# Node tiles in staged groups of four with index work behind them, an accumulator that holds x, and a selector multiplied in four pieces

## Chip, core and metric

The kernel runs on one core of a Trainium2 chip. The metric is device time in microseconds of one launch. Before the change it is 4528.94 us, the median of 10 runs (4525.16 to 4532.39). The names of the engines in the profile: PE multiplies matrices (PEld loads its weights), DVE is the vector engine, ACT the scalar engine, POOL is GpSimd, SP only issues DMAs. SP, ACT and POOL each have queues for DMAs.

## The reference

A layer of a graph network on 12,500 nodes (160 features: 64 scalars and 32 vectors of 3) and 400,000 edges, sorted by destination. Cut to what matters:

```
h  = max(layernorm(x), 0)
y0 = h[:, :64] @ W_l1_0 * a / 8 ;  y1 = einsum('nuc,uv->nvc', h1, W_l1_1) * a / sqrt(32)
s0, s1 = the same with W_sc0, W_sc1          # a: one factor per node
w  = silu(edge_features @ fc_W1 / 4) @ fc_W2 / 8    # 192 weights per edge
mid_a = w_a*y0[src]*e0 ; mid_d = w_d*sum_c(y1[src]*e1)/sqrt(3)
mid_b = (w_b*y0[src])[:, :, None]*e1 ; mid_c = (w_c*e0)[:, :, None]*y1[src]
z0, z1 = sums of mid over the edges of each destination / sqrt(10)
out = x + C_S*s + C_X*(z @ W_l2 * a / sqrt(96))
```

## The kernel before

The program has four parts in a row. Line numbers are those of the profile.

**Index work (L93 to L152).** Edges come in 3125 tiles of 128, three tiles to a window and four windows to a group (261 groups). `dst` is loaded and turned into floats (L103), the smallest destination of each window is found by a reduction (L107) and a POOL reduction over partitions (L112), and from that come the base tile of each group (`tile_i`), the positions `at`, and `drel`, the destination within its window (L114 to L149, all on DVE). A second POOL reduction (L151) makes `far_i`, which says whether a slow path for far destinations must run; with this data it is not entered. Weights are loaded by ACT's queue and scaled on DVE (L156 to L192).

**Node tiles (L220 to L256).** 98 tiles of 128 nodes in groups of 7. Per tile: row statistics on DVE (L231, L232), normalization on DVE (L240 for scalars, L242 for vectors, which are put in the order component, channel), two transposes on PE (L246, L247), the Relu in the copies out of PSUM (L249 on ACT, L250 on DVE), two matmuls against `wn0` and `wn1`, which hold both weight matrices side by side (L252, L253), and two copies: `yb` on ACT with the factor a (L254), and the other half into `acc` on DVE (L255). `yb` is written to `y_d` in DRAM by SP's queue (L256). A scheduler of the framework orders this part on each engine.

**Edges (L277 to L464).** The order is written out by hand, in steps b of four edge tiles (782 steps). `load` issues the gathers on POOL, one indirect DMA for each edge tile (L310), eight steps ahead, into ten buffers `yg`. `weigh` makes the edge weights (L341 on PE, L262 and L263 on ACT). `products` multiplies them with the gathered rows on DVE (L268 to L275). `select` makes, once per group, the 0/1 selector of 12 tiles (L364) and its three copies times the edge's vector (L366, 1152 elements per partition). `sums` multiplies selector and products on PE (L385). `turn`, `linear` and `add` (L400, L409, L421) take a finished group through the output weights, and `accumulate` adds the result to two neighbouring tiles of `acc`, whose number is read from `tile_i` into a register (L426 to L429).

**Output (L558 to L566).** All of x is loaded again, `acc` is multiplied by a on ACT (L562), and added to x on DVE in two instructions (L563, and L565 with the vector order undone); ACT's queue writes the rows.

Of the kernel before, what the change touches and what calls it, by code (L numbers as in the profile page):

```python
# [10 lines left out]
F32 = mybir.dt.float32  # L11
# [23 lines left out]
GN = 7  # L35
# [6 lines left out]
def kernel(  # L42
# [45 lines left out]
    nc.vector.memset(eps, EPS)  # L88

# [4 lines left out]
    nc.sync.dma_start(src_sb, src)  # L94
# [3 lines left out]
    far_i = const.tile([P, 1], I32, name="far_i")  # L98
    full = T // WT
    with tc.tile_pool(name="idx", bufs=1) as ip:  # L100
        dst_i = ip.tile([P, TP], I32, name="dst_i")
        nc.sync.dma_start(dst_i, dst)
        nc.vector.tensor_copy(drel, dst_i)  # L103
        neg = ip.tile([P, NG * GW], F32, name="neg")
# [6 lines left out]
        negb = ip.tile([P, NG * GW], F32, name="negb")  # L111
        nc.gpsimd.partition_all_reduce(negb, neg, P, bass_isa.ReduceOp.max)  # L112
        first = ip.tile([P, NG], F32, name="first")
# [36 lines left out]
        farb = ip.tile([P, 1], F32, name="farb")  # L150
        nc.gpsimd.partition_all_reduce(farb, far, P, bass_isa.ReduceOp.max)  # L151
        nc.vector.tensor_copy(far_i, farb)  # L152
# [3 lines left out]
    w1 = const.tile([P, 2 * FC_H], F32, name="w1")  # L156
    nc.vector.memset(w1, 0.0)
    for i in range(P // FC_IN):
        nc.scalar.dma_start(w1[FC_IN * i:FC_IN * (i + 1), FC_H * (i % 2):FC_H * (i % 2 + 1)], fc_w1)
    w2 = const.tile([P, NW], F32, name="w2")  # L160
    for i in range(2):
        for to, of, m in ((0, 0, M0), (M0, 2 * M0, M1), (M0 + M1, M0, M0), (2 * M0 + M1, 2 * M0 + M1, M1)):
            nc.scalar.dma_start(w2[FC_H * i:FC_H * (i + 1), to:to + m], fc_w2[:, of:of + m])
    nc.vector.tensor_scalar(w2, w2, 1.0 / math.sqrt(FC_H), None, ALU.mult)

    wn0 = const.tile([M0, 2, M0], F32, name="wn0")
    nc.scalar.dma_start(wn0[:, 0, :], w_l1_0)
    nc.scalar.dma_start(wn0[:, 1, :], w_sc0)
    nc.vector.tensor_scalar(wn0[:, 0, :], wn0[:, 0, :], 1.0 / math.sqrt(M0), None, ALU.mult)
    nc.vector.tensor_scalar(wn0[:, 1, :], wn0[:, 1, :], C_S / math.sqrt(M0), None, ALU.mult)  # L170
    wn1 = const.tile([3 * M1, 2, 3 * M1], F32, name="wn1")
    nc.vector.memset(wn1, 0.0)
    for c in range(3):
        s = slice(M1 * c, M1 * (c + 1))
        nc.scalar.dma_start(wn1[s, 0, s], w_l1_1)
        nc.scalar.dma_start(wn1[s, 1, s], w_sc1)
    nc.vector.tensor_scalar(wn1[:, 0, :], wn1[:, 0, :], 1.0 / math.sqrt(M1), None, ALU.mult)
    nc.vector.tensor_scalar(wn1[:, 1, :], wn1[:, 1, :], C_S / math.sqrt(M1), None, ALU.mult)

    wo = const.tile([P, 3, D], F32, name="wo")  # L180
    nc.vector.memset(wo, 0.0)

    def o1(c):
        return slice(M0 + M1 * c, M0 + M1 * (c + 1))

    nc.scalar.dma_start(wo[0:M0 + M1, 0, 0:M0], w_l2_0)
    for rows, k, c in ((slice(96, P), 0, 0), (slice(0, 32), 1, 1), (slice(32, 64), 1, 2)):
        nc.scalar.dma_start(wo[rows, k, o1(c)], w_l2_1[M0:, :])
    for rows, k, c in ((slice(64, P), 1, 0), (slice(0, 64), 2, 1), (slice(64, P), 2, 2)):
        nc.scalar.dma_start(wo[rows, k, o1(c)], w_l2_1[0:M0, :])  # L190
    nc.vector.tensor_scalar(wo[M0:M0 + M1, 0, 0:M0], wo[M0:M0 + M1, 0, 0:M0], 1.0 / math.sqrt(3.0), None, ALU.mult)
    nc.vector.tensor_scalar(wo, wo, C_X / math.sqrt(10.0 * (M0 + M1)), None, ALU.mult)  # L192
# [3 lines left out]
    nc.sync.dma_start(a_sb, attr)  # L196

# [3 lines left out]
    def node_dma(g, n, dma):  # L201

        f = min(g + n, N // P) - g
        if f:
            dma(slice(g * P, (g + f) * P), slice(0, f), P)
        if f < n:
            dma(slice((g + f) * P, N), slice(f, f + 1), N - (g + f) * P)
# [5 lines left out]
    def load_x(pool, g, n):  # L213
        xt = pool.tile([P, GN, D], F32, name="xt")
        if g + n == NT and N % P:
            nc.vector.memset(xt[:, n - 1, :], 0.0)
        node_dma(g, n, lambda rows, t, p: nc.sync.dma_start(xt[:p, t, :], by_tile(x[rows, :])))  # L217
        return xt

    with (  # L220
        tc.tile_pool(name="nx", bufs=4) as nx,
        tc.tile_pool(name="nd", bufs=3) as nd,
        tc.tile_pool(name="nd_pt", bufs=3, space=PSUM) as nd_pt,
        tc.tile_pool(name="nd_po", bufs=3, space=PSUM) as nd_po,
    ):
        for g, n in groups:
            xt = load_x(nx, g, n)
            st = nd.tile([P, GN, 6], F32, name="st")
            mv = nd.tile([P, GN, 2], F32, name="mv")
            for j in range(n):  # L230
                nc.vector.bn_stats(st[:, j, :], xt[:, j, :])  # L231
                nc.vector.bn_aggr(mv[:, j, :], st[:, j, :])  # L232
            rstd = nd.tile([P, GN], F32, name="rstd")
            nc.scalar.activation(rstd[:, :n], mv[:, :n, 1], AF.Sqrt, bias=eps)
            nc.vector.reciprocal(rstd[:, :n], rstd[:, :n])
            yb = nd.tile([P, GN, D], F32, name="yb")
            for j in range(n):
                i = g + j
                h = nd.tile([P, D], F32, name="h")
                nc.vector.tensor_scalar(h[:, 0:M0], xt[:, j, 0:M0], mv[:, j, 0:1], rstd[:, j:j + 1],  # L240
                                        ALU.subtract, ALU.mult)
                nc.vector.tensor_scalar(h[:, M0:].rearrange("p (c u) -> p c u", c=3),  # L242
                                        xt[:, j, M0:].rearrange("p (u c) -> p c u", c=3),
                                        mv[:, j, 0:1], rstd[:, j:j + 1], ALU.subtract, ALU.mult)
                pt = nd_pt.tile([P, 2, P], F32, name="pt")
                nc.tensor.transpose(pt[0:M0, 0, :], h[:, 0:M0], ident)  # L246
                nc.tensor.transpose(pt[0:3 * M1, 1, :], h[:, M0:], ident)  # L247
                hT = nd.tile([P, 2, P], F32, name="hT")
                nc.scalar.activation(hT[0:M0, 0, :], pt[0:M0, 0, :], AF.Relu)  # L249
                nc.vector.tensor_scalar(hT[0:3 * M1, 1, :], pt[0:3 * M1, 1, :], 0.0, None, ALU.max)  # L250
                po = nd_po.tile([P, 2, D], F32, name="po")
                nc.tensor.matmul(po[:, :, 0:M0], hT[0:M0, 0, :], wn0, start=True, stop=True)  # L252
                nc.tensor.matmul(po[:, :, M0:], hT[0:3 * M1, 1, :], wn1, start=True, stop=True)  # L253
                nc.scalar.activation(yb[:, j, :], po[:, 0, :], AF.Copy, scale=a_sb[:, i:i + 1])  # L254
                nc.vector.tensor_copy(acc[:, i, :], po[:, 1, :])  # L255
            node_dma(g, n, lambda rows, t, p: nc.sync.dma_start(by_tile(y_d[rows, :]), yb[:p, t, :]))  # L256
# [20 lines left out]
    with (  # L277
        tc.tile_pool(name="ld", bufs=2) as ld,
        tc.tile_pool(name="yg", bufs=10) as ygp,
        tc.tile_pool(name="hid", bufs=4) as hid,  # L280
        tc.tile_pool(name="prod", bufs=3) as prod,
        tc.tile_pool(name="selp", bufs=3) as selp,
# [75 lines left out]
        def select(g):  # L358

            ev = e4_group(g)  # L360
            lo, hi = g * TG, min((g + 1) * TG, T)
            n = hi - lo
            sel = selp.tile([P, TG, 4, WN], F32, name="sel")
            nc.vector.tensor_tensor(sel[:, :n, 3, :], iota[:, 0:WN].unsqueeze(1).to_broadcast([P, n, WN]),  # L364
                                    drel[:, lo:hi].unsqueeze(2).to_broadcast([P, n, WN]), ALU.is_equal)
            nc.vector.tensor_tensor(sel[:, :n, 0:3, :], sel[:, :n, 3:4, :].to_broadcast([P, n, 3, WN]),  # L366
                                    ev[:, :n, 1:4].unsqueeze(3).to_broadcast([P, n, 3, WN]), ALU.mult)
            sels[g] = sel
# [55 lines left out]
        def accumulate(g):  # L424
# [3 lines left out]
            to = acc[:, ds(i, 2), :]  # L428
            nc.vector.tensor_tensor(to, to, ps, ALU.add)  # L429
# [39 lines left out]
    with (  # L469
# [11 lines left out]
        with tc.For_i(0, n, 1) as _:  # L481
# [61 lines left out]
            with tc.For_i(0, NT, 1) as i:  # L543
# [11 lines left out]
                nc.vector.tensor_tensor(to, to, po.unsqueeze(1), ALU.add)  # L555


    with tc.tile_pool(name="fx", bufs=6) as fx:  # L558
        for g, n in groups:
            xt = load_x(fx, g, n)  # L560
            for j in range(n):
                nc.scalar.activation(acc[:, g + j, :], acc[:, g + j, :], AF.Copy, scale=a_sb[:, g + j:g + j + 1])  # L562
            nc.vector.tensor_add(xt[:, :n, 0:M0], xt[:, :n, 0:M0], acc[:, g:g + n, 0:M0])  # L563
            xv = xt[:, :n, M0:].rearrange("p t (u c) -> p t u c", c=3)
            nc.vector.tensor_add(xv, xv, acc[:, g:g + n, M0:].rearrange("p t (c u) -> p t u c", c=3))  # L565
            node_dma(g, n, lambda rows, t, p: nc.scalar.dma_start(by_tile(out[rows, :]), xt[:p, t, :]))  # L566
# [42 lines left out]
```

## Time and profile before

The profiled execution took 4524.6 us, of which its span, from first to last instruction, is 4522.7.

| | busy us | share | instructions |
|---|---|---|---|
| PE | 3544.0 | 78% | 17263 |
| DVE | 2791.1 | 62% | 6412 |
| ACT | 2567.4 | 57% | 9298 |
| POOL | 3230.5 | 71% | 3135 |

Busy time is an average over the four parts. The part with gathers runs from 284 to 4458 us, so what holds there is read from the rows of that stretch; the DMA engines moved 72 GB/s over the span and are far from full outside the last part. [...] Idle time "<-issue" is time in which an engine waited for nothing that the profile shows.

### The profile page before, as it was taken

Reading aid. Unit: us, or ns where it says so; the run is one execution under the profiler, and the core shown is the slowest. Engines: PE = TensorE matmul, PEld = TensorE weight load, DVE = VectorE, ACT = ScalarE, POOL = GpSimd, SP = SyncE. Lnnn points to the kernel's source line nnn. Section 1 sums busy time; section 2 is a strip of 40 time slices with the busy share of each in tenths; the row PEclk is TensorE's granted clock in tenths of the full one; section 3 lists DMA queues with packets and bytes.
Section 4 is the critical chain, followed back from the end, with each engine's and each line's share of the span. In section 5 each row is a group of like instructions: output and inputs, shape, how many; then the busy total and the mean of one; then the engine's idle time right before and its main releaser. Section 6 shows DMA issues by size and latency. Waiting matters only on the chain. (4 is left out here: it accounts for less than half of the span.)

```text
span 4522.7 us, 60313 instructions
## 1 busy us (share of the span) xinstructions
PE 3544.0 (78%) x17263; PEld 2454.8 (54%) x17263; DVE 2791.1 (62%) x6412; ACT 2567.4 (57%) x9298; POOL 3230.5 (71%) x3135
## 2 busy tenths in 40 slices
PE   4888887887787878787787777878878787877883
PEld 3555555555555555555555555555555555555552
DVE  6656666666666666666666666666666666666665
ACT  1245655655565556565655556555655565556555
POOL 0037777777777777777777777777777777777773
PEclk9999989899999999999989999889999999999997
DMA  2222222222222222222222222222222222222225
GB/s 82 71 61 71 71 69 69 70 68 71 69 71 71 70 69 71 68 71 71 69 70 71 69 70 71 68 70 69 72 71 70 69 71 68 71 70 69 70 67 170
DMA packets 245943, 327.78 MB, mean 72 GB/s; under 512 B 66040, under 2 KB 195352, under 8 KB 245352
## 3 DMA queue, kind: packets, MB, share of 16 engines
q0 software_dynamic: 150000, 256.20, 23.7%
q1 hardware_dynamic: 81030, 59.43, 4.5%
q10 hardware_dynamic: 14578, 8.25, 0.6%
q8 instruction: 141, 2.31, 0.2%
q14 instruction: 194, 1.59, 0.1%
HBM read 307.62 MB, written 16.00 MB: 72 GB/s over the span
## 5 line engine op out<-in xcount | busy, mean ns | idle before, releaser
L310 POOL DMA_INDIRECT yg<-y_d,src_sb x3125 | 3222.7, 1031 | 1188.0 <-issue 924.0
L385 PE MATMUL pz<-pr,sel 128*128 128x256 f32 x6250 | 1713.3, 422 | 678.6 <-DVE pr L275 676.6
L385 PEld LDWEIGHTS pz<-pr,sel 128*128 128x128 f32 x6250 | 1249.7, 210 | 955.1 <-DVE pr L275 545.6
L268 DVE TENSOR_TENSOR tmp<-yg,ev 128x384 f32<-128x384 f32 x782 | 436.3, 558 | 1544.4 <-DMA yg<-y_d,src_sb 1540.9
L262 ACT ACTIVATE wt<-pw,ev 128x96 f32<-128x96 f32 x3125 | 808.7, 344 | 324.3 <-ACT zs L392 213.6
L390 ACT ACTIVATE zs<-pz 32x192 f32<-32x192 f32 x1042 | 336.9, 323 | 1006.8 <-PE pz L385 999.8
L341 PE MATMUL pw<-w,hT 64*128 64x192 f32 x6250 | 778.6, 371 | 0.2 <-ACT wt L263 0.2
L341 PEld LDWEIGHTS pw<-w,hT 64*128 64x128 f32 x6250 | 532.6, 200 | 397.0 <-issue 395.9
L392 ACT ACTIVATE zs<-pz 32x64 f32<-32x64 f32 x3126 | 667.5, 214 | 41.6
L270 DVE TENSOR_REDUCE tmp<-tmp 128x128 f32<-128x384 f32 x782 | 463.8, 593 | 27.1
L319 PE MATMUL px<-xe,w 32*128 32x512 f32 x782 | 338.4, 710 | 158.1 <-DVE acc L429 156.8
L273 DVE TENSOR_TENSOR pr<-wt,yg 128x384 f32<-128x384 f32 x782 | 430.3, 550 | 0.0
L324 ACT ACTIVATE hT<-px 128x512 f32<-128x512 f32 x391 | 219.3, 595 | 343.1 <-PE px L319 339.7
L263 ACT ACTIVATE wt<-pw 128x384 f32<-128x384 f32 x782 | 398.9, 510 | 0.0
L366 DVE TENSOR_TENSOR sel<-sel,ev 128x1152 f32<-128x1152 f32 (+1 forms) x261 | 353.7, 1355 | 14.3 <-DMA ev<-in_e 5.4
L271 DVE TENSOR_TENSOR pr<-wt,yg 128x256 f32<-128x256 f32 x782 | 326.1, 417 | 0.0
L272 DVE TENSOR_TENSOR pr<-wt,yg 128x256 f32<-128x256 f32 x782 | 326.0, 417 | 0.0
L409 PE MATMUL px<-wo,za 128*128 128x160 f32 x1566 | 283.1, 317 | 0.4 <-ACT za L402 0.4
L409 PEld LDWEIGHTS px<-wo,za 128*128 128x128 f32 x1566 | 220.2, 190 | 60.1 <-ACT zs L392 33.7
L319 PEld LDWEIGHTS px<-xe,w 32*128 32x128 f32 x782 | 86.2, 201 | 285.9 <-DVE acc L429 210.0
L275 DVE TENSOR_TENSOR pr<-wt,tmp 128x128 f32<-128x128 f32 x782 | 223.2, 285 | 0.0
L421 PE MATMUL px<-os,place 128*128 128x160 f32 x1044 | 214.5, 328 | 0.4 <-ACT os L411 0.4
(78 smaller groups left out, 1736.9 us busy)
## 6 DMA issues: line engine op xcount, KB each, us to landing
yg<-y_d,src_sb POOLq DMA_INDIRECT x3125
xe<-in_e SPq DMA_DIRECT2D x784, 32.0 KB
xt<-in_x SPq DMA_DIRECT2D x26, 560.0 KB
y_d<-yb SPq DMA_DIRECT2D x13, 560.0 KB
out<-xt ACTq DMA_DIRECT2D x13, 560.0 KB
ev<-in_e SPq DMA_DIRECT2D x32, 192.0 KB
src_sb<-in_src SPq DMA_DIRECT2D x1, 1568.0 KB
dst_i<-in_dst SPq DMA_DIRECT2D x1, 1568.0 KB
```

What stands on the lines that cost most here:

```text
L262: nc.scalar.activation(wt[:, k, 0:96], pw[:, k, 0:96], AF.Copy, scale=ev[:, k, 0:1])
L263: nc.scalar.activation(wt[:, :n, 96:NW], pw[:, :n, 96:NW], AF.Copy)
L268: nc.vector.tensor_tensor(tmp[:, :n, 0:3, :], y1, ev[:, :n, 1:4].unsqueeze(3).to_broadcast([P, n, 3, M1]), ALU.mult)
L270: nc.vector.tensor_reduce(tmp[:, :n, 3, :], tmp[:, :n, 0:3, :].rearrange("p t c u -> p t u c"), AX.X, ALU.add)
L273: nc.vector.tensor_mul(pr[:, :n, 96:192].rearrange("p t (c u) -> p t c u", c=3), wt[:, :n, M0:96].unsqueeze(2).to_broadcast([P, n, 3, M1]) ...
L310: nc.gpsimd.indirect_dma_start(out=yg[:, k, :], out_offset=None, in_=y_d, in_offset=bass.IndirectOffsetOnAxis(ap=src_sb[:, t:t + 1], axis=0))
L319: nc.tensor.matmul(ph, w1[r, :], xe[r, :], start=True, stop=True)
L341: nc.tensor.matmul(pw[:, k, 0:NW], hT[r, o:o + P], w2[r, :], start=True, stop=True)
L366: nc.vector.tensor_tensor(sel[:, :n, 0:3, :], sel[:, :n, 3:4, :].to_broadcast([P, n, 3, WN]), ev[:, :n, 1:4].unsqueeze(3).to_broadcast([P, ...
L385: nc.tensor.matmul(pz[:, 0:PC], sels[g][:, t % TG, :, :], pr[:, k, :], start=t % WT == 0, stop=last)
L392: nc.scalar.activation(zs[:, 192 + M0 * c:192 + M0 * (c + 1)], pz[WN * c:WN * (c + 1), 192:PC], AF.Copy)
L409: nc.tensor.matmul(po[:m, :], za[:, k, :m], wo[:, k, :], start=k == 0, stop=k == 2)
```

## The change

Five things. The node part becomes stages of four tiles with an order written by hand (`center`, `leave`, `map_rows`, `turn_rows` of four different stages in one iteration, 25 stages); the normalization is split, so that ACT subtracts the mean with the Relu, and the factor 1/deviation, times a, comes at the very end. The index work and the edge weights move: x is loaded first, the first index pass is done in stage 6, and the rest after the last stage. `acc` starts as x + a s in the order of the output (the weights' columns are permuted), sums are added with the factor a, and the output part is DMAs alone, on two queues. The second POOL reduction becomes a matmul. The selector's multiplication runs in four pieces of three tiles. The pools `selp` and `prod` are made first.

```diff
-GN = 7
+GN = 8
+HN = 4
...
+        def center(q):
+            for k in range(n):
+                nc.vector.bn_stats(st[:, k, :], xt[:, j + k, :])
+                nc.vector.bn_aggr(mv[:, k, :], st[:, k, :])
+            nc.vector.tensor_scalar(nm[:, :n], mv[:, :n, 0], -1.0, None, ALU.mult)
+            for k in range(n):
+                nc.scalar.activation(h[:, k, :], xt[:, j + k, :], AF.Relu, bias=nm[:, k:k + 1])
+            nc.scalar.activation(ra[:, :n], mv[:, :n, 1], AF.Sqrt, bias=eps)
+        def turn_rows(q):
+            nc.vector.reciprocal(ra[:, :n], ra[:, :n])
+            nc.vector.tensor_mul(ra[:, :n], ra[:, :n], a_sb[:, g + j:g + j + n])
+            for k in range(n):
+                nc.tensor.transpose(pt[0:M0, 0, k, :], h[:, k, 0:M0], ident)
+                nc.tensor.transpose(pt[0:3 * M1, 1, k, :], h[:, k, M0:], ident)
+        def map_rows(q):
+            nc.scalar.activation(hT[0:M0, 0, :n, :], pt[0:M0, 0, :n, :], AF.Copy)
+            nc.vector.tensor_copy(hT[0:3 * M1, 1, :n, :], pt[0:3 * M1, 1, :n, :])
+            for k in range(n):
+                nc.tensor.matmul(po[:, :, 0:M0], hT[0:M0, 0, k, :], wn0, start=True, stop=True)
+                nc.tensor.matmul(po[:, :, M0:], hT[0:3 * M1, 1, k, :], wn1, start=True, stop=True)
+        def leave(q):
+            for k, po in enumerate(pos):
+                nc.scalar.activation(yb[:, j + k, :], po[:, 0, :], AF.Copy, scale=ra[:, k:k + 1])
+                nc.vector.scalar_tensor_tensor(acc[:, g + j + k, :], po[:, 1, :], ra[:, k:k + 1], xt[:, j + k, :],
+                                               op0=ALU.mult, op1=ALU.add)
...
+            for g, n in groups[:2]:
+                load_x(g, n)
+            nc.sync.dma_start(a_sb, attr)
+            node_weights()
+            nc.sync.dma_start(dst_i, dst)
...
+            for q in range(len(parts) + 3):
...
+                if q == min(2, last):
+                    edge_weight_loads()
+                if q == min(6, last):
+                    first_nodes()
+                if q <= last:
+                    center(q)
+                if 0 <= q - 3 <= last:
+                    leave(q - 3)
+                if 0 <= q - 2 <= last:
+                    map_rows(q - 2)
+                if 0 <= q - 1 <= last:
+                    turn_rows(q - 1)
+            edge_weights()
+            relate(pt[0:1, 0, 0, 0:1])
...
-            nc.vector.tensor_tensor(sel[:, :n, 0:3, :], sel[:, :n, 3:4, :].to_broadcast([P, n, 3, WN]),
-                                    ev[:, :n, 1:4].unsqueeze(3).to_broadcast([P, n, 3, WN]), ALU.mult)
+            for t in range(0, n, WT):
+                m = min(WT, n - t)
+                nc.vector.tensor_tensor(sel[:, t:t + m, 0:3, :], sel[:, t:t + m, 3:4, :].to_broadcast([P, m, 3, WN]),
+                                        ev[:, t:t + m, 1:4].unsqueeze(3).to_broadcast([P, m, 3, WN]), ALU.mult)
...
-            to = acc[:, ds(i, 2), :]
-            nc.vector.tensor_tensor(to, to, ps, ALU.add)
+            for h in range(2):
+                to = acc[:, ds(i + h, 1), :]
+                nc.vector.scalar_tensor_tensor(to, ps[:, h:h + 1, :], a_sb[:, ds(i + h, 1)], to,
+                                               op0=ALU.mult, op1=ALU.add)
...
-    with tc.tile_pool(name="fx", bufs=6) as fx:
-        for g, n in groups:
-            xt = load_x(fx, g, n)
...
+    for i, (g, n) in enumerate(groups):
+        eng = (nc.sync, nc.scalar)[i % 2]
+        node_dma(g, n, lambda rows, t, p: eng.dma_start(by_tile(out[rows, :]), acc[:p, g + t.start:g + t.stop, :]))
```

`first_nodes` holds L103 to L112 of before, `relate` the rest of the index work with the same instructions, `edge_weight_loads` the 23 loads of the edge part's weights on SP's queue, `edge_weights` their scalings on DVE. In the iteration each name is called for its stage: statistics and Relu of q, transposes of q − 1, copies and matmuls of q − 2, results of q − 3, whose second half of eight tiles also issues the write of `yb` to `y_d` on the queue of ACT.

## The prediction

> **What bounds the kernel now.** I read the stages first. In the table by stretch, each row is a stretch of the span with its length, then busy us (and instructions) of PE, weight loads, DVE, ACT, POOL, the clock column, DMA share and GB/s. The borders come from the timeline: first row statistics of a node tile at 52.36, last `yb` ended at 281.51, first gather at 284.08, last gather ended at 4458.46, first `xt` load of the closing loop at 4469.92.
>
> ```profile
> 0.00:52.30 52.30, 0.00 (x0) 0.00 (x0) 33.29 (x42) 0.00 (x0) 7.88 (x10) 1.00 0.26 85
> 52.30:281.50 229.20, 196.73 (x589) 129.29 (x590) 139.57 (x602) 68.75 (x211) 0.00 (x0) 1.00 0.22 65
> 284.10:4458.50 4174.40, 3338.45 (x16637) 2320.24 (x16637) 2591.37 (x5718) 2460.91 (x8974) 3222.64 (x3125) 0.92 0.29 70
> 4458.50:4470.00 11.50, 7.25 (x36) 5.25 (x36) 6.00 (x20) 4.29 (x16) 0.00 (x0) 1.00 0.04 9
> 4470.00:4522.70 52.70, 0.00 (x0) 0.00 (x0) 20.56 (x29) 32.65 (x98) 0.00 (x0) 0.50 0.99 304
> ```
>
> Index work alone takes 52 us, node tiles 229, edges 4174, output 53. Next come the costly groups: L310 is the gather of 128 rows of `y_d`, L366 the selector's multiplication.
>
> ```profile
> L310 POOL DMA_INDIRECT yg<-y_d,src_sb x3125 | 3222.7, 1031 | 1188.0 <-issue 924.0
> L366 DVE TENSOR_TENSOR sel<-sel,ev 128x1152 f32<-128x1152 f32 (+1 forms) x261 | 353.7, 1355 | 14.3 <-DMA ev<-in_e 5.4
> ```
>
> POOL's idle time before gathers is 1188 us: 236 is the wait for the first one, 924 is issue, about 0.30 per gather. So 3222.7 + 924 = 4147 of the 4174 us are gathers issued without a pause: **POOL bounds the edge stage**, and PE, busy 78%, waits for its rows. Now the mean of 1031 ns: half of all gathers take 0.94 or 0.95 us (median 946 ns). The slow ones are seen in the timelines of POOL and DVE side by side (start, us, engine, instruction):
>
> ```profile
> 1008.89 0.94 POOL L310 DMA_INDIRECT yg<-y_d,src_sb  x1 [0.30 <-issue]
> 1010.13 1.04 POOL L310 DMA_INDIRECT yg<-y_d,src_sb  x1 [0.30 <-issue]
> 1011.47 1.56 POOL L310 DMA_INDIRECT yg<-y_d,src_sb  x1 [0.30 <-issue]
> ```
>
> ```profile
> 1010.07 0.28 DVE L275 TENSOR_TENSOR pr<-wt,tmp 128x128 f32<-128x128 f32 x1
> 1010.27 0.55 DVE L364 TENSOR_TENSOR sel<-iota,drel 128x384 f32<-128x384 f32 x1
> 1010.85 1.36 DVE L366 TENSOR_TENSOR sel<-sel,ev 128x1152 f32<-128x1152 f32 x1
> ```
>
> The gather of 1011.47 begins inside L366, which ends at 1012.21, and finishes 0.82 us later. All such cases fit one rule: some 0.13 us after its start a gather needs something that a running DVE multiplication holds, and waits for that instruction's end. The gather of 1010.13 waits only for L275's end (1010.35, 0.09 us), though L364 follows without a gap: **the hold ends between two instructions**. Summing the time above 0.947 over all 3125 gathers by the DVE instruction running at that moment gives 263 us: L366 165 (269 gathers, 0.61 each), L273 41, L275 34, L268 17, L271 6, others under 2; the reduction L270 none.
>
> **Change 1: four pieces.** L366 (1152 elements, 1.36 us) becomes four of 288. By L271 (256 elements, 0.415 us, next start 0.33 later) and L273 (384, 0.55, 0.47) a piece takes 0.45 and the next starts 0.37 later: the train lasts 1.56 us, 0.2 more on a DVE busy 62% of this stage; it is hidden by DVE's 1541 us of waiting for rows. A gather now waits at most for one piece. Put at their present moments in L366, the gathers would wait 34 us in all instead of 165: gain 131. Evenly spread arrivals (0.2 us for 1.2 gathers in each of 261 groups) cost 68: gain 97. I take 115.
>
> Here a rule speaks against the change. The Trainium skill, "SBUF — State Buffer", section Who interferes with whom, says that a VectorE instruction with two SBUF inputs holds off GpSimd's reads, but infers that descriptor generation needs only the write side, so that a tensor_tensor did not stall such a DMA. By that, the gain is 0 and the sum 115 us higher. The 0.61 us rows decide for a hold.
>
> **Change 2: index work behind the node tiles.** Before, VectorE does it first, and the node tiles' row statistics wait until 52.36. After, the first x loads are SP's first issues, and eight small weight loads are ACT's. In the trace such issues take 0.45 to 0.8 us and land 1.7 later, so the four scalings queued in front of the first statistics on DVE end at about 8.5. Four statistics (0.29 per tile), four Relu (0.335, by L562), two table loads (1.28 each, one more than now), transposes and copies follow: the first matmul at about 16.9.
>
> **Change 3: stages of four.** What would one stage take? PE's rows now:
>
> ```profile
> 143.88 0.79 PE L252 MATMUL po<-wn,hT 64*128 64x128 f32 x2
> 144.60 1.01 PE L253 MATMUL po<-wn,hT 96*128 96x192 f32 x2
> 145.40 0.42 PE L246 MATMUL pt<-ident,h 128*64 128x128 f32 x1
> 145.62 0.42 PE L247 MATMUL pt<-ident,h 128*96 128x128 f32 x1
> ```
>
> A pair L252 costs 0.72 to the next start, a pair L253 0.80, or 0.94 where L252 comes again (0.46 instead of 0.32 at the switch, by 143.42 to 143.88); a transpose 0.213. In the new order the two pairs alternate: 3 × 1.66 + 1.52 = 6.5 us for four tiles, and eight transposes 1.71. The next stage's matmuls need the copies of the last transpose: 0.21 to its end, 0.05, ACT's copy of 64x512 0.59 (L249's 0.268 plus 384 elements), 0.06. Sum **9.1 us**. DVE and ACT lie beside it: statistics 1.4, Relu and Sqrt 1.6, four `yb` 1.25, add 0.35, copy 0.69, small ones 0.3: 5.5 us. Today four tiles take 229.2/98 × 4 = 9.35. So the stages gain almost nothing; the removed VectorE passes were not the bound. The index pass put into stage 6 (cast 1.78, reduction 3.41, memset 0.93) exceeds the slack by 2.9 once. The last matmuls start at 16.9 + 24 × 9.1 + 2.9 − 0.85, two tiles and `yb` follow, the last `yb` ends at 241.7. In the built program the first gather waits for the last `y_d` writes and the last add into `acc`, not for the index work: 2.6 us as now, 244.3 against 284.08. **Gain 40.**
>
> The clock is the open point. 0.213 us for 128 columns is half speed: in the edge stage eight L385 of 256 columns take 1.99 us, 0.216 to the next start, so 128 take 0.108. The clock column shows 1.00 only because no clock record exists before 289. The Trainium skill, "TensorE: Matmul & The Clock Gate", Part 1, has the clock doubled after one busy window of about 3.4 us; Part 4 adds that transposes don't count as busy. By the first alone, a stage would fall to the 5.5 us of DVE and ACT, and gathers start at about 161. But windows of this trace that are 83 to 91% full with transposes (as at 63.8 and 155.9) did not raise it; those that did in the edge stage were 77% or more in streaming columns, and the new matmul runs have only 1.07/1.66 = 64%. I take half speed.
>
> **What the move costs.** The second part of the index work and the scalings of `w2` and `wo` now run on DVE beside the first gathers, and it holds them as L366 does:
>
> ```profile
> 37.27 3.48 DVE L143 TENSOR_TENSOR over<-drel,lim 128x3123 f32<-128x3123 f32 x2
> 40.79 3.41 DVE L145 TENSOR_REDUCE far<-over 128x1 f32<-128x3125 f32 x1
> 44.12 3.40 DVE L147 SCALAR_TENSOR_TENSOR drel<-over,drel 128x3125 f32<-128x3125 f32 x1
> ```
>
> L142, L143 and L147 hold one gather each for 2.2 to 2.8 us, L123 for under 1: **cost 9** (0 to 15). It ends at about 265; the first products follow near 270. POOL may run ten blocks ahead, 53 us, to about 306, so it doesn't stop. The 23 edge weight loads queue on SP in front of the sixth x load, which is needed 38 us later; the `y_d` writes move from SP's queue to ACT's, 0.38 us of issue per eight tiles beside 3.6 of slack per stage; one POOL reduction (3.45) becomes a matmul while POOL has nothing else: nothing each.
>
> **Change 4: output.** The closing loop is gone: no x loads, scalings (ACT 32.7 us) or additions; its DMA share is 0.99. Left is 8 MB from `acc` by two queues. In the trace 14,578 packets of at most 640 bytes left by ACT's queue at about 32 ns each on 16 engines; 12,500 of them take 22 (at the peak of 358 GB/s) to 25 us. With 2.3 to the first byte and 0.5 at the end, 27 instead of 52.7: **gain 25.5**. The two dynamic adds of 160 for one of 320 (0.48) cost DVE about 0.5 per group, hidden as above, and 0.5 once at the end; whether their column of `a_sb` makes them hold gathers, no row shows: 0 to 21 us (261 × 0.08), I take 0, as L429 with one SBUF input costs nothing.
>
> **Sum.** 4522.7 − 40 + 9 − 115 − 25.5 + 0.5 = 4351.7 span; 1.9 lies around it (4524.6 − 4522.7): 4353.6. The median of the runs is 4.3 above the profiled run: **4358**.
>
> **Rivals.**
> - *The clock doubles in the node stage* (longer unbroken runs speak for it, the 91% window against): −83, so 4275.
> - *Stages don't overlap fully*, 11 us each (one hold of two buffers more than I see; L255 always waiting for `yb` shows such coupling): +46, 4404.
> - *Slower: gathers wait for the whole train of pieces.* Then 0.632 us per group becomes 0.835 (1.56/1.36 longer, and hit more often): +53, and if the dynamic adds hold too, +21. −40 + 9 − 25.5 + 0.5 + 74 = +18: 4547. It decides once pieces and adds cost over 56 us. The gather at 1010.13 speaks against it.
> - *The train holds, the adds don't*: 4526, no change.
>
> **Numbers.** Forecast 0.67 (own range 4315 to 4400: gain 97 to 131 on the pieces, 0.5 us either way per stage, contention 0 to 15, adds 0 to 21), clock 0.10, overlap 0.15, no change 0.03, slower 0.05. About 0.2% (9 us) can be told from no change. Range 4290 to 4415.
>
> **What would show it.** Gathers near the selector at 1.0 to 1.2 instead of 1.56; the sum of gathers near 3110 us; node matmul starts 9.1 us apart per stage; first gather near 244; three gathers of 3 us or more just after it; 27 us of output. Wrong if POOL pauses for `yg`, or if stages come at 5.5 or 11.

## The result and the profile after

The changed kernel takes 4414.83 us, the median of 8 runs (4408.60 to 4419.22), against 4528.54 for the kernel before (28 runs). The ratio is 0.9748, with a 95% interval of 0.9740 to 0.9757: faster, by 114 us where I forecast 171. That is inside my whole range (4290 to 4415) by 0.2 us, and outside the range of the forecast's own path, which ended at 4400. The profiled execution has a span of 4413.0.

In the table by stretch (columns as before: stretch, length, then busy us and instructions of PE, weight loads, DVE, ACT, POOL; clock, DMA share, GB/s) the borders are the first matmul of the node tiles, the first gather at 306.20, the last gather's end, and the start of the output's transfers:

```profile
19.00:304.00 285.00, 204.56 (x580) 133.14 (x580) 98.85 (x371) 75.23 (x231) 3.56 (x2) 1.00 0.17 50
306.20:4372.00 4065.80, 3300.21 (x16641) 2307.46 (x16641) 2739.55 (x6783) 2460.44 (x8973) 3114.06 (x3125) 0.92 0.30 72
4383.00:4413.00 30.00, 0.00 (x0) 0.00 (x0) 0.32 (x1) 0.00 (x0) 0.00 (x0) 0.53 0.91 268
```

| | before | after | forecast |
|---|---|---|---|
| first gather | 284.1 | 306.2 | 244.3 |
| from first gather to last gather's end | 4174.4 | 4065.8 | 4068.4 |
| from there to the end | 64.3 | 41.0 | 39.3 |

The edge part and the output came as forecast. The whole miss of 61 us is in front of the first gather: the gathers start 22 us later than before instead of 40 earlier.

The groups of the gather and of the selector's multiplication (busy, mean ns of one; then idle time before and what ended most of it):

```profile
L393 POOL DMA_INDIRECT yg<-y_d,src_sb x3125 | 3114.1, 997 | 1046.8 <-issue 898.7
...
L451 DVE TENSOR_TENSOR sel<-sel,ev 128x288 f32<-128x288 f32 x1042 | 407.5, 453 | 8.9
```

POOL is still the bound: 4065.8 − 3114.1 leaves 951.7 us between 3125 gathers, 0.30 each, which is issue; none waits for a buffer (the longest pause between two is 0.32 us, before the change as after it). The excess over 0.947 us, summed as before by the DVE instruction that holds the gather, fell from 263.3 to 154.7 us. The selector's line holds 278 gathers for 45.9 us, where it held 269 for 165.0. One of them, on POOL, and the train of four pieces that it falls into, on DVE:

```profile
365.31 1.22 POOL L393 DMA_INDIRECT yg<-y_d,src_sb  x1 [0.30 <-issue]
```

```profile
364.89 1.56 DVE L451 TENSOR_TENSOR sel<-sel,ev 128x288 f32<-128x288 f32 x4
```

The pieces start some 0.37 us apart and take 0.45, so the second ends at 365.71, and the gather ends 0.82 us after that, at 366.53. Held to the end of the train (366.45), it would have ended at 367.27.

Now the node part. PE's timeline shows the end of one stage's work and the start of the next (start, us, engine, instruction, idle time before and its releaser), and ACT's timeline the same moment:

```profile
111.35 0.42 PE L274 MATMUL pt<-ident,h 128*64 128x128 f32 x1
111.56 0.42 PE L275 MATMUL pt<-ident,h 128*96 128x128 f32 x1
115.79 0.79 PE L287 MATMUL po<-wn,hT 64*128 64x128 f32 x2 [3.81 <-ACT hT L282]
116.52 1.01 PE L288 MATMUL po<-wn,hT 96*128 96x192 f32 x2
117.45 0.79 PE L287 MATMUL po<-wn,hT 64*128 64x128 f32 x2
```

```profile
112.02 1.38 ACT L262 ACTIVATE h<-xt,nm 128x160 f32<-128x160 f32 x4 [8.51 <-PE pt L275]
113.31 0.28 ACT L264 ACTIVATE ra<-mv,eps 128x4 f32<-128x4 f32 x1
113.49 1.21 ACT L299 ACTIVATE yb<-po,ra 128x160 f32<-128x160 f32 x4
114.74 0.37 ACTq L304 DMA_DIRECT2D y_d<-yb  x1
115.15 0.59 ACT L282 ACTIVATE hT<-pt 64x512 f32<-64x512 f32 x1 [0.44 <-ACT yb L299]
```

The Relu (L262) waits 8.5 us, and its releaser is the last transpose (L275). `h` comes from the pool `nd`, which has two buffers. The Relu of stage q therefore writes where stage q − 2 lay, and the transposes of q − 2 are the last thing that PE does in the iteration before. Only then does ACT start: four Relus, the square root, four `yb`, a DMA issue, and at the end the copy (L282) for which PE waits. ACT's 3.7 us lie behind PE's 8.2, not beside them: a stage takes 11.7 or 12.2 us, not 9.1. The changed kernel itself shows what it would be otherwise. Near the end of the node part no new Relu is issued, ACT is free when the transposes end, and PE's pause shrinks to 0.68 us, with 9.10 us from stage to stage:

```profile
291.63 0.79 PE L287 MATMUL po<-wn,hT 64*128 64x128 f32 x2 [0.68 <-ACT hT L282]
```

### The profile page after: what moved, and what is told of

Its sections match the earlier page's. It is cut to its first block, busy times and chain, and to the rows that moved or that the text cites. A ratio compares the mean times of both kernels' runs of the same rounds, so it can differ in the third digit from the quotient of the medians.

```text
span 4413.0 us, 61941 instructions
## 1 busy us (share of the span) xinstructions
PE 3513.9 (80%) x17265; PEld 2447.2 (55%) x17265; DVE 2854.4 (65%) x7216; ACT 2548.8 (58%) x9237; POOL 3119.3 (71%) x3137
## 3 DMA queue, kind: packets, MB, share of 16 engines
q0 software_dynamic: 150000, 256.20, 24.3%
## 4 chain that ended last, share of the span: by engine, by line
POOL 44%; issue 30%; DMA 10%; DVE 6%; PE 3%; ACT 0%; DVEq 0%; POOLq 0%; ACTq 0%
POOL yg L393 44%; DMA yg<-y_d,src_sb 10%; PE pz L470 1%; DVE tmp L351 1%; DVE pr L354 1%; DVE pr L356 1%; DVE sel L451 1%; DVE pr L358 1%; DVE pr L355 1%; DVE acc L515 1%; PE pw L424 0%; PE po L288 0%; DVE tmp L353 0%; PE px L402 0%; DVE sel L447 0%
## 5 line engine op out<-in xcount | busy, mean ns | idle before, releaser
L393 POOL DMA_INDIRECT yg<-y_d,src_sb x3125 | 3114.1, 997 | 1046.8 <-issue 898.7
L470 PE MATMUL pz<-pr,sel 128*128 128x256 f32 x6250 | 1683.9, 417 | 586.9 <-DVE pr L358 585.2
L451 DVE TENSOR_TENSOR sel<-sel,ev 128x288 f32<-128x288 f32 x1042 | 407.5, 453 | 8.9
```

Of the source, the lines that this page charges most:

```text
L393: nc.gpsimd.indirect_dma_start(out=yg[:, k, :], out_offset=None, in_=y_d, in_offset=bass.IndirectOffsetOnAxis(ap=src_sb[:, t:t + 1], axis=0))
L451: nc.vector.tensor_tensor(sel[:, t:t + m, 0:3, :], sel[:, t:t + m, 3:4, :].to_broadcast([P, m, 3, WN]), ev[:, t:t + m, 1:4].unsqueeze(3).t ...
L470: nc.tensor.matmul(pz[:, 0:PC], sels[g][:, t % TG, :, :], pr[:, k, :], start=t % WT == 0, stop=last)
```

## The experiments

Runs e1 to e11 fell on three other chips (e1 to e4, e5 to e8, e9 to e11), where the kernel before takes 5350.58, 5333.44 and 5436.24 us; so their times are compared within a chip, and their stages by the trace. e12 fell on a chip like the first.

**e1 and e5: three buffers for h.**

```diff
+        tc.tile_pool(name="nh", bufs=3) as nh,
-            h = nd.tile([P, HN, D], F32, name="h")
+            h = nh.tile([P, HN, D], F32, name="h")
```

> The changed kernel with three buffers for h instead of two, nothing else. Theory (the Relu of stage q waits until PE has transposed stage q-2, so that Relu 1.4, Sqrt 0.2, the four yb 1.2 and the copy 0.6 run one after another behind PE in each stage): PE's idle time before each stage's matmuls falls from 3.3 to about 0.7, a stage from 11.7-12.2 to 9.1 us, the first gather from 306 to about 244, the time by 60 us to about 4355. Rival (four po buffers and the add that waits for yb tie the stages together): stages stay within 0.5 us of 11.7, the time within 12 us of 4415.

> The changed kernel with three buffers for h instead of two, nothing else. If the two buffers of h put the scalar engine's chain in series with the transposes (my theory), the node stage's period falls from 11.7 to 9.1 us and the first gather from 306 to 246 us, and since the gathers run behind one another from there the time falls by the same 60 us: 4355 us (4340 to 4370). If the gathers wait for something else as well (rival), the first gather comes at 246 us and the time stays above 4390.

The stage takes 9.10 us in both, and the first gather comes at 246.5 and 246.8. PE's timeline of e1:

```profile
112.36 0.42 PE L275 MATMUL pt<-ident,h 128*64 128x128 f32 x1
112.58 0.42 PE L276 MATMUL pt<-ident,h 128*96 128x128 f32 x1
113.68 0.79 PE L288 MATMUL po<-wn,hT 64*128 64x128 f32 x2 [0.68 <-ACT hT L283]
```

PE's pause is 0.68 us instead of 3.81: with a third buffer the wait is gone. The times are 5355.62 (ratio to before 1.0008, 0.9980 to 1.0036) and 5354.28 (1.0038, 1.0011 to 1.0064). That of e1 fits neither its theory nor its rival, and that of e5 is as its rival had it: on these chips the edge part isn't the gathers' alone. From e5, the stretch with gathers and the gather's group:

```profile
246.80:5269.40 5022.60, 3544.35 (x16458) 2513.49 (x16458) 2696.45 (x6716) 2453.10 (x8870) 3153.46 (x3125) 0.81 0.24 58
```

```profile
L394 POOL DMA_INDIRECT yg<-y_d,src_sb x3125 | 3153.5, 1009 | 1948.6 <-DVE pr L359 971.5
```

A gather costs nearly what it did (1009 ns against 997), but POOL now waits for the products that free its buffers (`pr` L359): its pauses between gathers exceed the 0.30 us of issue by 917 us in all.

**e2: two buffers, the Relu last.** `center(q)` is moved from the front of the iteration to its end, behind the transposes of q − 1.

```diff
-                if q <= last:
-                    center(q)
...
                     turn_rows(q - 1)
+                if q <= last:
+                    center(q)
```

> The changed kernel with two buffers for h, but with the statistics and the Relu of stage q put last in the iteration, behind results, copies and transposes of the earlier stages. Theory of the Relu's place: ACT's yb and copy are no longer queued behind a Relu that waits for PE, so a stage takes 9.1 to 9.5 us with two buffers too, the first gather comes at 245 to 255, the time near 4358. Rival (po and the add): no change, 4415.

The stage takes 9.10 us and the first gather comes at 244.2. So it is not the number of buffers as such, but that the waiting Relu stood in ACT's queue in front of the copy. Both runs keep the four `po` buffers and the add, so the rival that e1 and e2 share is out. The time is 5357.35 (1.0001, 0.9977 to 1.0025).

**e3, e4 and e7: the pieces alone.** e3 is the changed kernel with the multiplication in one piece; e4 and e7 are the kernel before with four pieces.

```diff
-            for t in range(0, n, WT):
-                m = min(WT, n - t)
-                nc.vector.tensor_tensor(sel[:, t:t + m, 0:3, :], sel[:, t:t + m, 3:4, :].to_broadcast([P, m, 3, WN]),
-                                        ev[:, t:t + m, 1:4].unsqueeze(3).to_broadcast([P, m, 3, WN]), ALU.mult)
+            nc.vector.tensor_tensor(sel[:, :n, 0:3, :], sel[:, :n, 3:4, :].to_broadcast([P, n, 3, WN]),
+                                    ev[:, :n, 1:4].unsqueeze(3).to_broadcast([P, n, 3, WN]), ALU.mult)
```

> The changed kernel with the selector's multiplication in one piece again. Theory (a gather is held until a running two-input DVE instruction ends): gathers held at that line lose about 0.6 us each again, their sum rises from 3114 by 105 to 125 us, the time to 4520-4540. Rival (the gathers became faster since the dynamic adds or other timing of DVE changed): under 40 us more.

> The kernel before with the selector's multiplication in four pieces, nothing else. Theory: the edge stage falls from 4174 to 4060-4075 us, the time from 4528 to 4412-4425, which is what the whole change gives, so that its other parts sum to nothing. Rival (the pieces pay only together with the later start or the new adds): over 4460.

> The kernel before with the selector's multiplication in four pieces and nothing else of the change. If a gather is held until the running instruction of the vector engine ends, and no longer (theory), the sum of the gathers falls by 110 us to 3110 and the time to 4420 us (4405 to 4435). If gathers wait for the whole train of pieces (rival), the sum stays within 20 us of 3223 and the time above 4510.

In one piece the line holds 258 gathers for 70.0 us (sum of gathers 3208); in four, 325 for 30.8 (e4, sum 3159) and 330 for 34.3 (e7, 3161). A hold per gather of 0.27 us in one piece and 0.10 in four: the direction is the theory's, but the gathers have pauses here, so that the sizes are not those of the first chip. On e3's own chip, e1 and e2, which keep the four pieces, have 24.3 and 26.1 us at this line. The times of e3, e4 and e7 are 5385.24 (1.0050, 1.0024 to 1.0075), 5403.92 (1.0082, 1.0054 to 1.0111) and 5413.77 (1.0136, 1.0092 to 1.0181). Four pieces alone make the kernel slower on these chips, by 0.8 and 1.4%, against the theory of e4 and e7. e3 points the same way: from the first gather to the last one's end it takes 5002.6 us in one piece, where e1 and e2 take 5036.8 and 5031.1 in four. Why is not shown. No run has the pieces alone on a chip like the first; what they are worth there rests on the sums of the two traces above.

**e6 and e11: three buffers, and the node matmuls grouped by their weights.**

```diff
                 nc.tensor.matmul(po[:, :, 0:M0], hT[0:M0, 0, k, :], wn0, start=True, stop=True)
-                nc.tensor.matmul(po[:, :, M0:], hT[0:3 * M1, 1, k, :], wn1, start=True, stop=True)
                 pos.append(po)
+            for k, po in enumerate(pos):
+                nc.tensor.matmul(po[:, :, M0:], hT[0:3 * M1, 1, k, :], wn1, start=True, stop=True)
```

> As the kernel with three buffers for h, and a node stage multiplies its four tiles by the one weight matrix, then its four tiles by the other. If the price of a tile's pair of matmuls (1.66 us) is the change of weights at each of them (theory), four tiles take 4.6 us instead of 6.5: a period of about 7.2 us, the first gather at 200 us and a time of 4310 us. If the price is that of streaming the columns alone (rival), the period stays at 9.1 us and the time at 4355. If the fuller TensorE also doubles its clock in the node stage (second rival), the period falls under 6.5 us and the first gather comes before 180 us.

> Three buffers for h and the node stage's matmuls grouped by their weights, nothing left out. First gather at 194 us. If the start of the gathers moves the end by as much where TensorE runs undisturbed (theory), the time is 4304 us (4290 to 4320); on a chip that holds TensorE back it is about 0.995 of that of the kernel before, as TensorE sets the end there (theory), and not 0.95 (rival, by which the gathers set it there too).

Two stages in a row of e6, on PE:

```profile
108.15 2.07 PE L288 MATMUL po<-wn,hT 64*128 64x128 f32 x8 [3.18 <-ACT hT L283]
110.16 2.93 PE L291 MATMUL po<-wn,hT 96*128 96x192 f32 x8
112.87 0.42 PE L275 MATMUL pt<-ident,h 128*64 128x128 f32 x1
...
115.12 1.16 PE L288 MATMUL po<-wn,hT 64*128 64x128 f32 x8 [0.68 <-ACT hT L283]
116.20 1.57 PE L291 MATMUL po<-wn,hT 96*128 96x192 f32 x8
117.61 0.27 PE L275 MATMUL pt<-ident,h 128*64 128x128 f32 x1
```

Four tiles take 4.72 us from 108.15 to the first transpose, near the 4.6 expected from fewer changes of weights. In the next stage they take 2.49: the clock has doubled, as the second rival had it, and it falls back afterwards. Stages take 6.7 and 7.0 us in turn, now set by DVE and ACT, as the pause of 3.18 before the slow stage shows. First gather at 194.1 and 193.4. The times are 5308.62 (0.9952, 0.9922 to 0.9983) and 5402.63 (0.9934, 0.9911 to 0.9957). Against e5 on the same chip that is 45.7 us less for a start 52.7 us earlier. On a chip like the first it was not run.

**e8: three buffers, twelve pieces.** The loop over pieces makes one for each tile (128x96).

> As the kernel with three buffers for h, with the selector's multiplication in twelve pieces of 128x96, one for each tile, instead of four of 128x288. If a hold ends with the instruction it began in (theory), a gather that falls on a piece is held by half of 0.25 us instead of half of 0.45, but more gathers fall on pieces, since twelve take about 3 us of the vector engine and four take 1.8: an excess of about 35 us at that line instead of 46, 4345 us. If the vector engine's added 310 us decide instead (rival), the gathers wait for buffers and the time is above 4400.

The line holds 417 gathers for 291.8 us, not 35; in four pieces, in e5 on the same chip, it holds 320 for 25.2. POOL's and DVE's timelines:

```profile
433.28 2.20 POOL L394 DMA_INDIRECT yg<-y_d,src_sb  x1 [0.31 <-issue]
```

```profile
432.08 2.11 DVE L451 TENSOR_TENSOR sel<-sel,ev 128x96 f32<-128x96 f32 x12
434.11 0.55 DVE L352 TENSOR_TENSOR tmp<-yg,ev 128x384 f32<-128x384 f32 x1
434.69 0.60 DVE L354 TENSOR_REDUCE tmp<-tmp 128x128 f32<-128x384 f32 x1
```

The gather begins inside the train and ends 0.82 us after L352, at 435.48: it was held through the rest of the pieces, 0.17 us apart, and through the multiplication behind them, until the reduction came. That refutes the general form of my rule. The time is nevertheless 5267.35 (0.9855, 0.9810 to 0.9901), the shortest on its chip, where the gathers don't set the end; why it is shorter than e5 is not shown.

**e9 and e10: two tiles of three left out of the sums,** with two buffers for h and with three.

```diff
-                nc.tensor.matmul(pz[:, 0:PC], sels[g][:, t % TG, :, :], pr[:, k, :], start=t % WT == 0, stop=last)
+                if t % WT == 0:
+                    nc.tensor.matmul(pz[:, 0:PC], sels[g][:, t % TG, :, :], pr[:, k, :], start=True, stop=True)
```

> The changed kernel, where two of a window's three tiles are left out of the sums: their matmul with the selector isn't issued, so that TensorE does some 1950 us less (1120 of matmuls, 825 of weight loads beside them), and everything else, gathers, selectors and products, is done. If the gathers' engine sets the end of the edge stage (theory), leaving this work out moves little where TensorE runs undisturbed, and frees the stage of TensorE where that is held back: 4415 us (4380 to 4430), first gather 306 us. If another engine sets it (rival), the time stays above 4800 on a chip that takes 5340 for the kernel before.

> The same with three buffers for h instead of two; the same matmuls of the sums are left out. If the start of the gathers moves the end by as much (theory), the first gather comes at 246 us and the time is 60 us below that of the run with two buffers and the same matmuls left out (50 to 70). If the edge stage takes the gain back (rival), the two times differ by less than 20 us.

5434.54 and 5375.94 us. The first gathers come at 305.9 and 246.3, 59.6 us apart, and the times differ by 58.6: the edge part gives nothing of the start back (5057.1 and 5058.3 from first to last gather). That e9 stayed above 4800 says that something other than the gathers sets the end there, and that a quarter of PE's matmul instructions fewer (13099 for 17265) doesn't change it. The clock fell with them: in the part with gathers it is 0.69 in e9, against 0.81 in e5.

**e12: the changed kernel again.**

> The changed kernel itself, nothing left out. On a chip that takes some 4530 us for the kernel before: 4415 us, a ratio of 0.975. On a chip that takes some 5350 us for it, where the results of TensorE come late: by my theory the gain of the gathers is not to be had there, as they wait for the other engines, and what is left is the later start of the gathers against the kernel before (306 us instead of 284), less the shorter end; from the run with three buffers for h (1.0008 to 1.0038) plus 60 us it is a ratio of 1.012 to 1.015. By the rival, that the change is worth the same everywhere, it is 0.975 there too.

4415.19 us, 0.9744 (0.9722 to 0.9765), on another chip where before takes 4530.46. First gather 305.8, stages of 11.68 and 12.2 us: the result repeats. What the change is worth on the other chips stays untested.

## Why the forecast was half right

- **POOL bounds the edges, and gathers are held by running multiplications:** right. The stage fell by exactly what the excess fell, 108.6 us.
- **Four pieces, gain 115:** 165.0 − 45.9 = 119. The rest of the excess rose by 10.5, of which 6.3 are the index work below. So the inference that the prediction set against the change, that such a multiplication doesn't stall a gather, does not hold here.
- **Index work beside the first gathers, cost 9:** right in kind, 6.3 in size. POOL's timeline has the three gathers, and POOL did not pause after them:

```profile
314.59 3.02 POOL L393 DMA_INDIRECT yg<-y_d,src_sb  x1 [0.30 <-issue]
317.91 3.14 POOL L393 DMA_INDIRECT yg<-y_d,src_sb  x1 [0.30 <-issue]
...
325.11 3.01 POOL L393 DMA_INDIRECT yg<-y_d,src_sb  x1 [0.30 <-issue]
```

- **Output, gain 25.5 less 0.5:** 23.3. The transfers take 30 us at a DMA share of 0.91, not 27.
- **First matmul at 16.9:** 19.05.
- **Index pass in stage 6, 2.9 over the slack:** that stage takes 13.2 us, 1.0 more than its like; in e1, where stages take 9.1, it is 4.1 more.
- **The stage of four at 9.1 us, with "DVE and ACT lie beside it":** this step failed. Its PE terms were right to a few hundredths (two pairs 1.66, eight transposes 1.71), and e1, e2, e5 and e10 show 9.10 with a first gather at 244 to 247, as the step put it. But in the kernel as it stood ACT did not lie beside PE. I had added up each engine's busy time and the one dependence from transpose to copy. I had not asked which buffer the Relu writes, and who reads it last. The rival "one hold of two buffers more than I see" named this at 11 us a stage and 4404, with a chance of 0.15, and it is what came; only its size was low by 0.7 to 1.2 us a stage. That the time still lies in my range is luck.
- **The clock in the node stage:** half speed, as taken: of 172 intervals between neighbouring transposes of the changed kernel, 170 are 0.21 us. That it can double there, e6 shows.

The miss adds up: 306.2 − 244.3 = 61.9 in front, −2.6 in the edge part, +1.7 behind, together 61.0 of span. Of the part in front, 2.1 is the first matmul, and the stages make up the rest: from the first stage's matmuls to the last one's pass 280.6 us, where the forecast has 24 × 9.1 + 2.9 − 0.85 = 220.5 and e1 takes 221.4. Two slips in the working changed nothing: evenly spread arrivals come to 0.2 × 1.2 × 261 = 63 us, not 68, and the work of DVE and ACT in a stage to 5.6, not 5.5. My estimate for a kernel with three buffers for h on the first chip is some 4355 us (4413 − 60, + 1.8). e10 supports that, but it was not run there.

## What to carry to other kernels

For a pipeline written by hand, list for each tile its buffers, the stage whose reader frees the one that is written next, and what stands in the writing engine's queue behind that write. Sums of busy time say "beside" where a two-buffer tile says "after". When a bound engine is slowed by others' instructions, split the longest of those, but measure each size: four pieces brought the holds of one line from 165 us to 46, while on the chip of e5 and e8 twelve brought 292 where four had 25.

## What the hardware showed unexpectedly

**Late results of TensorE.** On the three chips with 5330 to 5440 us, 1200 to 1300 of some 3660 matmuls of the edge part that signal their end (3340 in e9 and e10) do so more than 1 us after the modelled end, counting the first signal after each one's start; on the chips with 4530 us, 5 to 9. In e5:

```profile
572.26 0.81 PE L507 MATMUL px<-os,place 128*128 128x160 f32 x4
572.90 1.89 PE L471 MATMUL pz<-pr,sel 128*128 128x256 f32 x8
574.73 0.92 PE L425 MATMUL pw<-w,hT 64*128 64x192 f32 x8
580.91 1.18 PE L486 MATMUL px<-ident,zs 128*128 128x128 f32 x3 [5.27 <-ACT zs L476]
```

```profile
578.79 0.80 DVE L516 SCALAR_TENSOR_TENSOR acc<-px,a_sb,acc 128x160 f32 x2 [8.15 <-remote]
```

The sum of L507 was to end at 573.07, but DVE gets it at 578.79. PE looks idle for 5 us in which its results are still to come. PE spends some 1950 us of e5 at half clock, against 658 for the changed kernel on the first chip. In e9, with a quarter fewer matmuls but more time at half clock (3188 us), as many are late, so the number of matmuls alone isn't the cause; the cause stays open.

**When the clock doubles, and that transposes count.** In these traces the clock changes at multiples of 3.41 us, so the node stage can be cut into such stretches, in step with its changes. I count as full the time in which columns are streamed, 0.213 us for 128 at half speed. In e6, stretches that were 0.96 full or more, transposes counted, were followed by the doubled clock; the next two were some 0.65 and 0.32 full, and it fell back. In the changed kernel the fullest are 0.80, and it never rose there. Two stretches of e6, each with the one after it (columns as in the tables by stretch, the clock third from the end):

```profile
110.53:113.94 3.41, 3.41 (x13) 3.17 (x13) 1.42 (x7) 2.69 (x9) 0.00 (x0) 0.50 0.63 192
113.94:117.35 3.41, 2.73 (x19) 2.36 (x18) 2.39 (x11) 0.59 (x1) 0.00 (x0) 1.00 0.01 2
175.38:178.79 3.41, 3.41 (x14) 3.19 (x13) 0.94 (x5) 0.79 (x2) 0.00 (x0) 0.50 0.43 138
178.79:182.21 3.42, 2.74 (x12) 2.03 (x11) 1.39 (x4) 1.38 (x3) 0.00 (x0) 0.50 0.00 0
```

The first is 0.97 full, 0.66 with matmuls and the rest with transposes, and the clock doubled. The third is 0.91 full with the same matmuls and no transpose, and the clock stayed. All 11 rises in the node part of e6 are of the first kind, with 0.51 to 0.66 of matmuls, and e11 shows the same. If transposes did not count, the third should have raised the clock before the first. So they count here, against the second of the two rules that the prediction weighed, by which they don't. How full is full enough is open: before the change, in the edge part, 0.77 was once enough and 0.88 once not.

**The end of a hold.** Multiplications 0.37 us apart let a waiting gather through. At 0.17 us apart, in e8, by the piece that ran 0.13 us after the gather's start, 175 gathers in the eighth of twelve pieces were held 1.31 us on average, while 68 in the fourth were held 0.045. What decides between these is not known.
